# Ordering the additions of a mixture's output behind factors and scores on VectorE, at the start of an attention stage

## The chip, the cores and the metric

The kernel runs on one core of a Trainium2 chip. The metric is the device time of one execution in microseconds (us). The core has TensorE (PE in the profile, PEld for its weight loads), VectorE (DVE), ScalarE (ACT), GpSimd (POOL) and SyncE (SP); each works through its own queue of instructions in order.

## The reference, cut to what matters

The input `x` has 128 graphs of 64 nodes with 256 features, `adj` the edge weights. Two layers follow each other, each with a graph part and a feed-forward part that are added to `x`:

```python
x = x + _L0_gnn_ref(_layernorm(x, axis=-1), adj, ...)
x = x + _L0_ffn_ref(_layernorm(x, axis=-1), ...)      # 8 experts, the best one's output, times its probability
x = x + _L1_gnn_ref(_layernorm(x, axis=-1), adj, ...) # attention over a graph's 64 nodes
x = x + _L1_ffn_ref(_layernorm(x, axis=-1), ...)      # scores from 1,048,576 edges, then two of four experts
```

The change lies where the second line's sum meets the third line. Of the attention this is what counts here:

```python
Wh = jnp.matmul(h, W)
s1, s2 = Wh @ a1, Wh @ a2
e = s1[:, :, None] + s2[:, None, :]
e = jnp.where(e > 0, e, ALPHA * e)
e = jnp.where(adj > 0, e, NEG)
attention = jax.nn.softmax(e, axis=2)
h_prime = jnp.matmul(attention, Wh)
```

then a layer norm over the features and a gelu. `h` is the layer norm of `x`, so its mean and variance per node are needed before anything else of the attention can start.

## The kernel before, in words

The 8192 nodes are 64 tiles of 128 nodes by 256 features; `x` stays on chip as one array `[128, 64, 256]`. Four tiles make a group (`GR = 4`), so there are 16 groups (`NG`).

Layer 0's experts have written their rows to DRAM (`yrows`), in an order by expert. The function `back(g)` fetches the rows of a group's four tiles again with indirect DMAs issued by GpSimd (L1146, "gathers" here; one per tile, into tiles named `yin`, of which there are six, `by = GR + 2`), multiplies each with its node's probability and adds it to `x` (L1152, "additions" here), and takes the tile's statistics (L1138, `raw_stats`).

Layer 1's attention runs as a pipeline in steps `s`. In step `s` five functions work on five different groups, as generators that take turns: `back(s)`, `combine(s - 7)`, `tables(s - 10)`, `second(s - 5)` and `first(s - 4)`. With `PART = 2` the offsets are `FIRST = 4`, `SECOND = 5`, `COMBINE = 7`, `TABLES = 10`.

- `make_factors(i)` comes at the end of every second step. It turns the collected statistics of two steps into scales and shifts ("factors", tile `fac`): a chain of small VectorE instructions (L163 to L167, L1286, L154 to L159, L1290, L1291) of 128 x 24 elements. The first factors need the statistics of groups 0 and 1, the second those of groups 2 and 3.
- `first(g)` scales a group's tiles on ScalarE (L1037, tile `z`), transposes them on TensorE (L1168, `tz`), copies them (L1169, `zT`), multiplies by the weights (L1179, `pw`, copied to `wh` at L1182; L1186, `p2`), and makes the scores on VectorE (`ee`, five instructions, L1195 to L1208).
- `second(g)` does the softmax's exponential, a transpose and the product with `wh`, and takes statistics. `combine(g)` normalizes, applies gelu and adds to `x` (L1252). `tables(g)` prepares the second layer's feed-forward part, whose expert matrix products ("units", L1068 to L1082) are mixed in from step 12 on.

What is written above is the order in which the program is traced. The program's builder then makes each engine's queue from it: it plays the program through with durations of its own and puts, on each engine, an instruction that is ready before one that would have to wait, else the one traced earlier. So an addition of a later group can come to stand among the instructions of an earlier group's factors. `with tc.issue_after(ins):` tells the builder that the instructions traced inside, as far as they are on the engine of `ins`, have to come behind `ins` in that engine's queue. It adds no semaphore and no instruction. `made` is a dictionary in which the functions leave things for each other; `made["sent"]`, for instance, orders the loading of weights behind a step's store (L1316).

Of the kernel before, what the change touches and what calls it, by code (L numbers as in the profile page):

```python
# [15 lines left out]
ALU = mybir.AluOpType  # L16
# [4 lines left out]
P = 128  # L21
# [3 lines left out]
GR = 4  # L25
PART = 2


FIRST, SECOND, COMBINE, TABLES = 2 * PART, 2 * PART + 1, 3 * PART + 1, 4 * PART + 2
# [51 lines left out]
def kernel(  # L81
# [32 lines left out]
    V, S = nc.vector, nc.scalar  # L114
# [24 lines left out]
    x = const.tile([P, NT, D], F32, name="x")  # L139
# [12 lines left out]
    def root_of_bits(dst, v, guess, work):  # L152

        V.tensor_scalar(work.bitcast(I32), v.bitcast(I32), 1, None, ALU.logical_shift_right)  # L154
        V.tensor_scalar(guess.bitcast(I32), work.bitcast(I32), -1.0, float(0x5F3759DF), ALU.mult, ALU.add)
        for j in range(3):
            V.tensor_tensor(work, guess, v, ALU.mult)
            V.scalar_tensor_tensor(work, work, -0.5, guess, ALU.mult, ALU.mult)
            V.scalar_tensor_tensor(dst if j == 2 else guess, work, 1.5, guess, ALU.add, ALU.mult)  # L159

    def moments(raw, sm, df, var):

        V.tensor_tensor(sm, raw[:, :, :, 1], raw[:, :, :, 4], ALU.add)  # L163
        V.tensor_tensor(df, raw[:, :, :, 1], raw[:, :, :, 4], ALU.subtract)
        V.tensor_tensor(var, raw[:, :, :, 2], raw[:, :, :, 5], ALU.add)
        V.scalar_tensor_tensor(df, df, 0.25, df, ALU.mult, ALU.mult)
        V.scalar_tensor_tensor(var, var, 1.0 / D, df, ALU.mult, ALU.add)  # L167
# [21 lines left out]
    psel = const.tile([P, NT], F32, name="psel")  # L189
# [229 lines left out]
    with tc.tile_pool(name="w0", bufs=1, reuse_waits="tile") as w0, tc.tile_pool(name="kp", bufs=1, reuse_waits="tile") as kp:  # L419
# [29 lines left out]
        with tc.tile_pool(name="b2", bufs=2, reuse_waits="tile") as b2, tc.tile_pool(name="bh", bufs=NH + 2, reuse_waits="tile") as bh, tc.tile_pool(  # L449
# [4 lines left out]
            def transposed(zT, z, k):  # L454
                tz = psb.tile([P, GR * P], F32, name="tz")[:, 0:D].rearrange("p (c n) -> p c n", c=2)
                for c in range(2):
                    nc.tensor.transpose(tz[:, c, :], z[:, c * P : c * P + P], ident)
                S.copy(zT[:, :, k * P : k * P + P], tz)
# [16 lines left out]
            with tc.tile_pool(name="bg1", bufs=1, reuse_waits="tile") as bg1, tc.tile_pool(name="bg2", bufs=2, reuse_waits="tile") as bg2, tc.tile_pool(  # L475
# [58 lines left out]
                fac = bg1.tile([P, n_parts + 2, 4, M], F32, name="fac")  # L534
# [318 lines left out]
                V.tensor_tensor(past, past, tiles.unsqueeze(1).to_broadcast([P, NSLOT, E0]), ALU.mult)  # L853
                first = bg1.tile([P, NSLOT], F32, name="first")
                V.tensor_reduce(first, past, AX.X, ALU.add)
                V.tensor_tensor(iota_s, iota_s, first, ALU.subtract)
                V.scalar_tensor_tensor(es, es, float(NROW // P), iota_s, ALU.mult, ALU.add)
                V.tensor_scalar(es, es, 0.0, float(E0 * NROW // P - 1), ALU.max, ALU.min)
                last = V.tensor_copy(slot_t, es).ins

            with tc.tile_pool(name="bs", bufs=3, reuse_waits="tile") as bs, tc.tile_pool(
# [80 lines left out]
                for g in range(beside):  # L942
# [6 lines left out]
                    last = unit  # L949
# [166 lines left out]
    with ExitStack() as of_c:  # L1116
# [18 lines left out]
        made = {}  # L1135

        def raw_stats(norm, k, src):
            V.bn_stats(made["raw"][:, norm, s % PART * GR + k, :], src)  # L1138

        def back(g):  # L1140

            ys = []
            for k in range(GR):
                t = GR * g + k
                y = by.tile([P, D], F32, name="yin")
                nc.gpsimd.indirect_dma_start(  # L1146
                    y, None, yrows, bass.IndirectOffsetOnAxis(ap=row_y[:, t : t + 1], axis=0)
                )
                ys.append(y)
            for k in range(GR):  # L1150
                t = GR * g + k
                V.scalar_tensor_tensor(x[:, t, :], ys[k], psel[:, t : t + 1], x[:, t, :], ALU.mult, ALU.add)  # L1152
                raw_stats(0, k, x[:, t, :])
                yield

# [16 lines left out]
        def first(g):  # L1172
            zT = yield from transposed(g, 0)
            yield
            wh = whs[g % 2]
            for k in range(GR):
                pw = psc.tile([P, D + 1], F32, name="pw")
                for c in range(2):
                    nc.tensor.matmul(  # L1179
                        pw, zT[:, c, k * P : k * P + P], wx[:, c, :], start=(c == 0), stop=(c == 1)  # L1180
                    )
                S.copy(wh[:, k, 0 : D + 1], pw)  # L1182
            p2 = psc.tile([P, GR * P], F32, name="p2")
            for h in HALVES:
                for c in range(2):
                    nc.tensor.matmul(  # L1186
                        p2[h, 0 : GR * 64].rearrange("p (k j) -> p k j", j=64),
                        w2r[:, c, :],
                        zT[:, c, :].rearrange("p (k n) -> p k n", n=P)[:, :, h],
                        start=(c == 0),  # L1190
                        stop=(c == 1),
                    )
            yield
            ee = c2.tile([P, GR, 64], F32, name="ee")
            V.tensor_tensor(  # L1195
                ee,
                p2[:, 0 : GR * 64].rearrange("p (k j) -> p k j", j=64),
                wh[:, :, 0:1].to_broadcast([P, GR, 64]),
                ALU.add,
            )  # L1200
            V.scalar_tensor_tensor(ee, ee, 0.2, ee, ALU.mult, ALU.max)

            top = c1.tile([P, GR, 64], F32, name="top")
            V.tensor_scalar(top, on[:, GR * g : GR * g + GR, :], -2.0 * NEG, NEG, ALU.mult, ALU.add)
            V.tensor_tensor(ee, ee, top, ALU.min)
            m = c2.tile([P, GR], F32, name="m")
            V.tensor_reduce(m, ee, AX.X, ALU.max)
            V.tensor_tensor(ee, ee, m.unsqueeze(2).to_broadcast([P, GR, 64]), ALU.subtract)  # L1208
            made[g] = ee
            yield  # L1210

# [68 lines left out]
        def make_factors(i):  # L1280

            shape = [P, 3, PART * GR]
            raw = made["raw"]
            sm, df, ve, y, w = (c2.tile(shape, F32, name=f"mf{j}") for j in range(5))
            moments(raw, sm, df, ve)
            V.tensor_tensor(ve, ve, made["eps"], ALU.add)  # L1286
            fac = facs[i] = cf.tile([P, 3, 3, PART * GR], F32, name="fac")
            scale = fac[:, 0]
            root_of_bits(scale, ve, y, w)
            V.scalar_tensor_tensor(fac[:, 1], sm, -0.5, scale, ALU.mult, ALU.mult)  # L1290
            V.tensor_scalar(fac[:, 2], sm, 0.5, None, ALU.mult)  # L1291


        to.update(
# [9 lines left out]
        g, n = 0, -1  # L1304
        for s in range(n_steps):
            if s % PART == 0:
                made["raw"] = c2.tile([P, 3, PART * GR, 6], F32, name="raw")
                made["eps"] = c2.tile([P, 3, PART * GR], F32, name="eps")
                V.memset(made["raw"], 0.0)
                V.memset(made["eps"], EPS)  # L1310
            streams = []
            for of, by_steps in ((back, 0), (combine, COMBINE), (tables, TABLES), (second, SECOND), (first, FIRST)):
                if 0 <= s - by_steps < NG:
                    streams.append((of(s - by_steps), 2 if of == second and s % 2 else 0))
            if s == TABLES + 1:
                with tc.issue_after(made["sent"]):  # L1316
                    load_weights()

            r = 0
            while streams:  # L1320
                streams = [(st, at) for st, at in streams if at > r or next(st, s) is None]

                at = s - TABLES - 2
                if s >= NG + SECOND:
                    quota = int(r < 3)
                elif at >= 0:
                    quota = (2 * (at % 2), 2 * (at % 2), 4 - 4 * (at % 2), 0, 0, 0, 0, 0)[r]
                else:
                    quota = 0
                for _ in range(quota):  # L1330
                    g, n = next(units)
                r += 1
            if s % PART == PART - 1:
                make_factors(s // PART)
        while (n + 1) % (NH1 + GR):
            g, n = next(units)
# [255 lines left out]
    ahead = ctx.enter_context(tc.tile_pool(name="ahead", bufs=5, reuse_waits="tile"))  # L1592
# [354 lines left out]
    with tc.tile_pool(name="gd", bufs=1, reuse_waits="tile") as gd:  # L1947
        steps = gates(gd, 0, T0, {})
        for _ in sending:
            next(steps, None)  # L1950
            next(steps, None)
            g, n = next(units)
        for _ in steps:
            pass
        while (n + 1) % (NH1 + GR):
            g, n = next(units)
# [96 lines left out]
    with tc.tile_pool(name="fp", bufs=3, reuse_waits="tile") as fp:  # L2053


        moves = {0: send(1, sz), 1: back(0)}
        for n, h in enumerate(pairs()):
            if n % 3 == 2:
                next(moves[h], None)
            if n % 9 == 8:  # L2060
                next(stored, None)
    for _ in moves[1]:
        pass
    steps = back(PARTS - 1)
    for n, _ in enumerate(units):
        next(steps, None)
# [61 lines left out]
```

## Time and profile before

| | us |
|---|---|
| time before, median of 3 runs | 2247.34 (2247.14 to 2250.24) |
| the profiled execution: its own time | 2273.71 |
| its span, first to last instruction | 2272.0 |
| TensorE busy | 2081.2 (92%) |
| VectorE busy | 1522.8 (67%) |
| ScalarE busy | 921.7 (41%) |
| GpSimd busy | 448.6 (20%) |
| 64 gathers, L1146 | 64.3, from 1121.8 to 1305.6 |
| 64 additions, L1152 | 480 ns each (median), from 1125.5 to 1335.3 |

Times within the span count from its start. In the profile's lines, `x<-yin,psel,x` reads "writes x from yin, psel and x"; what stands in brackets after an instruction is how long its engine had been idle and what ended that. "remote" means that the profile has no sender for the semaphore that ended the wait; "issue" that it shows no wait at all. The attention stage starts at about 1118, and its last step's addition to `x` (L1252) is at 1479.7. The profiled execution is longer than the median of the runs by 26.4 us.

### The profile page before, as it was taken

The page shows a single profiled execution, that of the slowest core. Times are in us where ns is not written, and L with a number is a line of the kernel's source. Part 1 is how long each engine was busy: PE and PEld are TensorE (multiplying, and loading weights), DVE is VectorE, ACT ScalarE, POOL GpSimd, SP SyncE. Part 2 cuts the span into 40 slices and gives each one's busy share as a digit, 9 for nine tenths or more (in the row PEclk, how much of TensorE's full clock was granted, in tenths as well). Part 3 has the DMA queues.
Part 4 walks back from the last instruction along what each step waited for, and adds up shares of the span by engine and source line. Part 5 has one row for each costly group of instructions (what it writes and reads, how often), then busy time and mean ns, then how long its engine had stood idle before and what let it go on. Part 6 is the DMA issues. An engine that isn't in the chain of part 4 may idle for free. (4 is left out here: it accounts for less than half of the span.)

```text
span 2272.0 us, 31371 instructions
## 1 busy us (share of the span) xinstructions
PE 2081.2 (92%) x10046; PEld 1397.8 (62%) x10046; DVE 1522.8 (67%) x4539; ACT 921.7 (41%) x1662; POOL 448.6 (20%) x469
## 2 busy tenths in 40 slices
PE   7899999997999999999667889998999999999899
PEld 4444444443666666666445667665767767888776
DVE  6898988725899898893268665665788652323335
ACT  5767676663121121122046555531333342333322
POOL 2011101111000000000142200004556552213213
PEclk9999999998999999999878888998999999999999
DMA  8121112232111211112223311182222237878843
GB/s 223 31 68 59 49 55 68 83 98 77 55 35 53 61 32 54 54 32 72 59 67 103 95 33 43 66 245 62 60 57 50 58 117 219 281 239 263 251 144 105
DMA packets 206732, 219.84 MB, mean 97 GB/s; under 512 B 53200, under 2 KB 174416, under 8 KB 206560
## 3 DMA queue, kind: packets, MB, share of 16 engines
q1 hardware_dynamic: 181296, 182.37, 26.3%
q0 software_dynamic: 17056, 35.09, 5.6%
q8 instruction: 86, 1.41, 0.3%
q10 hardware_dynamic: 8208, 0.26, 0.2%
q14 instruction: 86, 0.70, 0.1%
HBM read 132.66 MB, written 84.91 MB: 96 GB/s over the span
## 5 line engine op out<-in xcount | busy, mean ns | idle before, releaser
L467 PE MATMUL ph<-zT,w 128*128 128x512 f32 x1056 | 507.2, 611 | 9.5 <-ACT zT L694 5.1
L470 ACT ACTIVATE hT<-ph,b 128x512 f32<-128x512 f32 x264 | 180.8, 687 | 501.0 <-PE ph L467 490.7
L467 PEld LDWEIGHTS ph<-zT,w 128*128 128x128 f32 x1056 | 190.1, 193 | 191.9 <-issue 168.8
L928 PE MATMUL py<-wd,hT 128*128 x1088 | 251.6, 383 | 0.0
L297 DVE TENSOR_TENSOR one<-iota_l,pb 128x1024 bf16<-128x1024 bf16 x192 | 234.3, 1220 | 1.2 <-PE cnt_ps L308 1.2
L928 PEld LDWEIGHTS py<-wd,hT 128*128 128x128 f32 x1088 | 200.8, 190 | 24.5 <-issue 0.5
L1540 POOL DMA_INDIRECT got<-tsrc,esrc x144 | 167.0, 1160 | 208.4 <-DVE esrc L1511 86.8
L1146 POOL DMA_INDIRECT yin<-yrows,row_y x64 | 64.3, 1005 | 693.7 <-SPq L991 573.3
L1078 PE MATMUL py<-w,hT 128*128 128x256 f32 x800 | 192.1, 391 | 9.1 <-DVE kt L1473 4.0
L1068 PE MATMUL ph<-zT,w 128*128 128x512 f32 x400 | 186.8, 609 | 0.0
L1078 PEld LDWEIGHTS py<-w,hT 128*128 128x128 f32 x800 | 150.9, 194 | 39.4 <-issue 13.9
L1072 ACT ACTIVATE hT<-ph,b 128x512 f32<-128x512 f32 x100 | 68.7, 688 | 212.5 <-PE ph L1068 193.6
L2004 PE MATMUL ph<-zTp,w1e 128*128 128x256 f32 x608 | 142.4, 389 | 12.2 <-DMA w1e<-in_L_ffn_W_dram 10.6
L2008 ACT ACTIVATE hT<-ph,b1e 128x256 f32<-128x256 f32 x152 | 71.7, 475 | 185.2 <-PE ph L2004 118.3
L2017 PE MATMUL py<-w,hT 128*128 x608 | 139.7, 383 | 2.8 <-DVE y L2025 2.5
L2004 PEld LDWEIGHTS ph<-zTp,w1e 128*128 128x128 f32 x608 | 118.4, 195 | 30.8 <-issue 11.9
L297 DVE TENSOR_TENSOR one<-iota_h,pb 128x512 bf16<-128x512 bf16 x192 | 131.7, 689 | 0.0
L620 PE MATMUL pre<-wd 128*128 128x512 f32 x256 | 126.9, 609 | 1.5 <-ACT wd L606 1.3
L1924 DVE SCALAR_TENSOR_TENSOR x<-yin,gate,x 128x256 f32<-128x256 f32 x108 | 52.1, 484 | 110.1 <-DMA yin<-ystore 105.4
L2017 PEld LDWEIGHTS py<-w,hT 128*128 128x128 f32 x608 | 113.8, 192 | 18.3 <-DVE y L2025 3.9
L308 PEld LDWEIGHTS <-one 128*128 128x128 bf16 x1536 | 69.4, 98 | 84.9 <-issue 59.7
L1068 PEld LDWEIGHTS ph<-zT,w 128*128 128x128 f32 x400 | 74.6, 194 | 73.2 <-issue 72.0
(414 smaller groups left out, 3468.6 us busy)
## 6 DMA issues: line engine op xcount, KB each, us to landing
w1e<-in_L_ffn_W_dram SPq DMA_DIRECT2D x38, 512.0 KB
yin<-ystore SPq DMA_DIRECT2D x24, 512.0 KB
ystore<-y SPq DMA_DIRECT2D x80, 128.0 KB
zslots<-none SPq DMA_DIRECT2D x38, 256.0 KB
zin<-zslots SPq DMA_DIRECT2D x38, 256.0 KB
yslots<-y SPq DMA_DIRECT2D x76, 128.0 KB
zin<-zrows SPq DMA_DIRECT2D x68, 128.0 KB
bd<-in_L_ffn_bd_dram SPq DMA_DIRECT2D x68, 128.0 KB
```

The costliest lines, as they stand in the source:

```text
L297: V.tensor_tensor(o, wi.unsqueeze(1).to_broadcast([P, HK, n]), pb[:, g : g + HK].unsqueeze(2).to_broadcast([P, HK, n]), ALU.is_equal,)
L308: nc.tensor.matmul(self.ps, one[0][:, k, :], one[1][:, k, :], start=(at + k == 0), stop=(at + k == n_chunks * KEPT - 1),)
L467: nc.tensor.matmul(ph, w1[:, c, q * P : q * P + P], zT[:, c, :], start=(c == 0), stop=(c == 1))
L470: gelus.append(S.activation(hT, ph, AF.Gelu, bias=b1[:, q : q + 1]).ins)
L620: nc.tensor.matmul(pre, xnT[:, c, n * P : n * P + P], wcat[:, c, :], start=(c == 0), stop=(c == 1),)
L928: nc.tensor.matmul(py, hTs[q][:, k * P : k * P + P], wd[:, bass.ds(ex[k], 1), q, :].rearrange("p e f -> p (e f)"), start=(q == 0), stop=(q ...
L1068: nc.tensor.matmul(ph, w1[:, e, c, q * P : q * P + P], zT[:, c, :], start=(c == 0), stop=(c == 1))
L1078: nc.tensor.matmul(py, hTs[q][:, k * P : k * P + P], w2[:, e, q, :], start=(q == 0), stop=(q == NH1 - 1))
L1540: nc.gpsimd.indirect_dma_start(got, None, tsrc, bass.IndirectOffsetOnAxis(ap=esrc[:, b, at : at + 1], axis=0))
L2004: nc.tensor.matmul(ph, w1e[:, c, q * P : q * P + P], zT[:, c, :], start=(c == 0), stop=(c == 1))
L2008: pace[:] = [S, S.activation(hT, ph, AF.Gelu, bias=b1e[:, q : q + 1]).ins]
L2017: nc.tensor.matmul(py, hTs[q][:, k * P : k * P + P], w2[:, e, q, :].rearrange("p e f -> p (e f)"), start=(q == 0), stop=(q == NH1 - 1),)
```

## The change

The additions of groups 2 to 8 are put under `issue_after`: those of groups 2, 3 and 4 behind the last factors traced so far, those of groups 5 to 8 behind the last scores traced so far. By the steps, that is the first factors for groups 2 and 3, the second for group 4, and the scores of group `g - 5` for group `g` from 5 to 8. Groups 0 and 1 and those from 9 on are left free. Two lines keep the instructions in `made`. The gathers are on GpSimd and get no order; but a gather needs one of six tiles, which an addition sets free.

```diff
@@ back(g), after its four gathers @@
+            if PART <= g <= FIRST:
+                ahead = made["factors"]
+            elif FIRST < g <= 2 * FIRST:
+                ahead = made["scores"]
+            else:
+                ahead = None
             for k in range(GR):
                 t = GR * g + k
-                V.scalar_tensor_tensor(x[:, t, :], ys[k], psel[:, t : t + 1], x[:, t, :], ALU.mult, ALU.add)
+                with tc.issue_after(ahead) if ahead is not None else ExitStack():
+                    V.scalar_tensor_tensor(x[:, t, :], ys[k], psel[:, t : t + 1], x[:, t, :], ALU.mult, ALU.add)
                 raw_stats(0, k, x[:, t, :])
                 yield
@@ first(g), the last of the score instructions @@
-            V.tensor_tensor(ee, ee, m.unsqueeze(2).to_broadcast([P, GR, 64]), ALU.subtract)
+            made["scores"] = V.tensor_tensor(ee, ee, m.unsqueeze(2).to_broadcast([P, GR, 64]), ALU.subtract).ins
@@ make_factors(i) @@
-            V.scalar_tensor_tensor(fac[:, 1], sm, -0.5, scale, ALU.mult, ALU.mult)
+            last = V.scalar_tensor_tensor(fac[:, 1], sm, -0.5, scale, ALU.mult, ALU.mult)
             V.tensor_scalar(fac[:, 2], sm, 0.5, None, ALU.mult)
+            made["factors"] = last.ins
```

## The prediction

> **What bounds the kernel now.** I read the engine windows first, then the waits, then the timeline of VectorE. Over the whole span TensorE is busy 92%, so only time in which it stands still can be won. The change touches one place, the start of layer 1's attention, and there TensorE does stand still. In the windows, the columns are PE, PEld, DVE, ACT and POOL busy (with counts), granted clock, DMA share, GB/s:
>
> ```profile
> core 0: us, PE busy (x) PEld busy (x) DVE busy (x) ACT busy (x) POOL busy (x), PEclk, DMA share, GB/s
> 1177.00:1220.00 43.00, 35.77 (x174) 25.21 (x172) 41.30 (x145) 33.88 (x71) 10.78 (x10) 0.92 0.11 32
> 1118.00:1177.00 59.00, 19.31 (x68) 11.74 (x69) 31.15 (x118) 13.18 (x27) 35.23 (x36) 0.62 0.30 87
> 1117.00:1149.20 32.20, 0.00 (x0) 0.00 (x0) 17.41 (x64) 0.63 (x2) 20.95 (x22) 0.58 0.33 96
> ```
>
> TensorE does nothing for 32.2 us (last row). POOL is then busy 20.95 us issuing 22 gathers. Further on, 1177 to 1220, VectorE is full: 41.30 of 43.00 us. The waits of 1118 to 1150 name who is waited for:
>
> ```profile
> ACT z L1037 <- DVE eps L1310: 44.7, 1, 44.7
> PE tz L1168 <- ACT z L1037: 32.3, 1, 32.3
> DVE x L1152 <- DMA yin<-yrows,row_y: 10.3, 9, 5.6
> ```
>
> TensorE's first transposes wait for ScalarE's scaling (L1037), and that for a memset (L1310) which stands just behind the last instruction of the first factors (L1290). So the factors are what is late. VectorE itself waited 10.3 us for gathers. Its timeline shows where:
>
> ```profile
> 1136.00 0.18 DVE L163 TENSOR_TENSOR mf<-raw 128x24 f32<-128x24 f32 x1
> ...
> 1137.46 0.48 DVE L1152 SCALAR_TENSOR_TENSOR x<-yin,psel,x 128x256 f32<-128x256 f32 x1 [0.40 <-DMA yin<-yrows,row_y]
> ...
> 1139.99 0.48 DVE L1152 SCALAR_TENSOR_TENSOR x<-yin,psel,x 128x256 f32<-128x256 f32 x1 [0.56 <-DMA yin<-yrows,row_y]
> ...
> 1142.57 0.48 DVE L1152 SCALAR_TENSOR_TENSOR x<-yin,psel,x 128x256 f32<-128x256 f32 x1 [0.62 <-DMA yin<-yrows,row_y]
> ...
> 1147.76 0.18 DVE L1290 SCALAR_TENSOR_TENSOR fac<-mf,fac 128x24 f32<-128x24 f32 x1 [1.75 <-remote]
> ```
>
> The factors of groups 0 and 1 start at 1136.00 and end at 1147.94. In between stand additions 9 to 15 (counted from 0), which belong to groups 2 and 3. Each is held until its gather lands, and gathers come one per 1.26 us (POOL starts at 1137.21, 1138.48, 1139.74).
>
> **What the Trainium skill says.** "DMA: Bandwidth & Descriptors", section "Anatomy of one DMA — SWDGE (gpsimd) path", gives a gather a fixed part of about 2.0 us plus its bytes; the trace agrees: the gather of 1125.69 is used by the addition at 1128.61, 2.9 us later, of which 1.1 us is POOL's own. "TensorE: Matmul & The Clock Gate", section "What's actually happening", says that TensorE runs at half clock after an idle window of about 3.4 us until it has been busy as long; the trace agrees (granted clock 0.58 in the idle row, 0.92 in the busy one). So an earlier start also ends the slow clock earlier; I count nothing extra for it.
>
> **The change, part by part.** No instruction is added or taken away. 28 of the 64 additions (groups 2 to 8) get an order on VectorE only. Groups 2 and 3 go behind the first factors, group 4 behind the second factors, groups 5 to 8 behind the scores of groups 0 to 3. All of these orders bind: by the windows of L1152, 9 additions ran before 1136, 7 more before 1147.9, 8 more before 1159.4 (end of the second factors), 2 before the first scores end (1164.4 begins the last of their instructions), 5 before the second's (1180.0), 2 and 4 before the third's and fourth's: 31 by 1180, 37 by 1200.2. Now at most 8 may run before the first factors end, 16 before the second, and 20, 24, 28 and 32 before the first, second, third and fourth scores.
>
> *First factors.* Addition 7 starts at 1133.72 and takes 0.48; its statistics (L1138, 0.42) end at about 1134.7. A chain of factors has 19 instructions. Undisturbed, its last ten run at 0.216 us each (a later chain in the timeline: 1492.76 to 1494.88). The first four depend on nothing in the chain and take 0.11 each, the other five I price like the last: 4 x 0.11 + 15 x 0.216 = 3.7. So they end at 1138.4 instead of 1147.94: **9.5 us earlier**, and TensorE's first transposes come at 1139.7 instead of 1149.2. If the 1.75 us stall before L1290 comes back, 7.8.
>
> *What waits behind.* Additions 8 to 13 run from 1138.4; their gathers have landed or are in flight. Gather 14 needs the buffer of addition 8 (six buffers), so 1139 at the earliest; it went at 1139.74 anyway. So POOL loses nothing here, and has no other work until 1441. SyncE gets no new wait. Addition 15 comes at about 1144, the second factors at 1144.5 + 3.7 = 1148.2 against 1159.4: 11.2 earlier. Additions of group 4 follow until 1151.3. The first scores need TensorE's chain, 1149.2 to 1164.8 before (15.6): now 1139.6 + 15.6 = 1155.2 at the latest, 9.6 earlier.
>
> *Additions behind scores.* These take work out of VectorE's idle stretch and put it into its full one. One addition with its statistics takes 0.40 + 0.37 = 0.77 at the pitch of 1191.6 to 1195.1. At the second scores 24 are done instead of 31 (7 late, 5.4 us); at the fourth 32 instead of 37 (5 late, 3.9 us). VectorE is 96% busy from 1177 to 1220, so the most that this can cost is 5.4. The least is nothing: from 1149.2 to 1177 VectorE idled 27.80 - 14.16 = 13.6 us, and if the scores follow each other quickly there is room for the moved work between them. Fillers also stretch the chain of five score instructions, from 2.1 us of work to 3.1 (1161.7 to 1164.8); without them each gets up to 1.0 back. I take 2 us of cost. The cover is idle VectorE time before step 7; without it the 5.4 applies.
>
> *Gathers.* They move with the buffers: group 5's third and fourth additions free buffers for group 6's last ones only after the first scores. A refill of two takes 2 x 1.26 + 2.9 = 5.4 us. The scores came 15.6, 10.7 and 9.5 us apart, so I cost this at nothing, 0 to 5 us.
>
> *Sum.* -9.5 + 2 = **-7.5 us**, between -11 (no cost, 11.2 at the second factors) and +1 (-7.8, +5.4, +3 for a late gather). The profiled execution took 2273.71 us (span 2272.0), 26.4 over the median of 2247.34; -7.5 makes it 2266. I put the same difference on the median, **2239.8**: the waits counted are mostly gathers' pitch, which is work of POOL. What the profile may add here are the stalls put down to "remote" (VectorE 5.4, ScalarE 7.2 us, all between 1146 and 1174), which I did not count as gained.
>
> **Does the head start last to the end?** The chain of waits reaches back only to 1548. After 1300 TensorE is busy 90.8 of 100 and then 95.4 of 100 us; nothing there has a date of its own, and the loading of weights (L1316) is itself ordered behind an attention step. So I let it shift whole.
>
> **The rivals.**
> *More than that.* The stalls of 1146 to 1174 lie in the thick of the gathers. If pacing gathers takes away some of them (ScalarE's 4.4 and 2.8), the gain is 9.5 + 7.2 less 0 to 2: 2231 to 2233. For it: they occur nowhere else. Against: VectorE's came while POOL idled, too. Chance 0.20.
> *About the same.* The program's builder orders all instructions by its own clock; a changed start reshuffles what follows, and a few us are given back between 1220 and 1300, where TensorE is busy 65.3 of 80: 2245. Chance 0.17.
> *Slower.* One mechanism: an addition behind scores stands in VectorE's order before its gather has landed, and the scores and statistics behind it wait. Its price is up to 5.4 us for each of groups 5 to 8; it decides once scores follow each other within 5.4 + 3.1 = 8.5 us. The gaps before were longer, but the first included stalls. Half of it in four groups is 11, with 5.4 for moved work, less 9.5: +7, 2254. Chance 0.17.
> *The order does not bind.* The counts above exclude it.
>
> **How the numbers follow.** My forecast, -7.5, has 0.46; with the larger gain, faster by over 0.2% (4.5 us, about what a measurement of this kernel can tell from no change) has 0.66. Same 0.17, slower 0.17. The range runs from the larger gain's 2231, a little below it, to the zero end of the sum and part of the slower case: 2230 to 2251. The likeliest case alone: 2236 to 2243.
>
> **What would show it.** Right: the first factors run without additions inside and end within 4 us of their start; the row L1152 <- DMA falls well below 10.3 us; TensorE's idle stretch is some 9 us shorter; 24 additions at the second scores. Wrong: additions of groups 5 to 8 waiting for DMA between 1155 and 1200 (the slower rival), or a later step such as L1252's last (1479.7) not moved by 5 us or more (head start lost).

## The result, and the profile after

| | before | after |
|---|---|---|
| median of 9 runs each, us | 2248.09 | 2240.14 |
| lowest to highest, us | 2244.28 to 2255.81 | 2233.34 to 2244.97 |
| ratio, 95% interval | | 0.9961 (0.9944 to 0.9978) |
| the profiled execution: time, span, us | 2273.71, 2272.0 | 2244.57, 2242.9 |

The kernel became 8.0 us faster in these runs. In two later sets of runs, on different chips, the full change came to 0.9974 as it is, and to 0.9966 with one transfer moved that turned out not to matter.

The page of the kernel after, its first lines:

```profile
span 2242.9 us, 31370 instructions
PE 2075.3 (93%) x10046; PEld 1394.6 (62%) x10046; DVE 1525.5 (68%) x4539; ACT 920.9 (41%) x1662; POOL 447.3 (20%) x469
```

The two spans differ by 29 us, but that is not the change: a second profile of the kernel before, shown below, has a span of 2243.5. The profile that the prediction rests on was a disturbed execution. So I read after against the second profile of before. The waits of before (second profile) from 1118 to 1146, columns engine, line and what is waited for, then us in total, times, longest:

```profile
ACT z L1037 <- DVE fac L1290: 40.9, 1, 40.9
PE tz L1168 <- ACT z L1037: 28.5, 1, 28.5
DVE x L1152 <- DMA yin<-yrows,row_y: 10.3, 11, 5.7
```

The waits of after from 1118 to 1140 (the added lines shift L1152 to L1161, L1168 to L1177, L1252 to L1261, L1290 to L1299):

```profile
ACT z L1037 <- DVE fac L1299: 34.6, 1, 34.6
PE tz L1177 <- ACT z L1037: 22.3, 1, 22.3
DVE x L1161 <- DMA yin<-yrows,row_y: 8.0, 5, 5.8
```

TensorE's wait fell from 28.5 to 22.3. VectorE still waits 8.0 us for gathers, but 5.8 of that is the first gather of all, which nothing could hide. Why TensorE waits less is in VectorE's timeline of after:

```profile
1134.84 0.20 DVE L163 TENSOR_TENSOR mf<-raw 128x24 f32<-128x24 f32 x1
...
1138.06 0.18 DVE L159 SCALAR_TENSOR_TENSOR fac<-mf,mf 128x24 f32<-128x24 f32 x1
1138.28 0.18 DVE L1299 SCALAR_TENSOR_TENSOR fac<-mf,fac 128x24 f32<-128x24 f32 x1
1138.38 0.87 DVE L1161 SCALAR_TENSOR_TENSOR x<-yin,psel,x 128x256 f32<-128x256 f32 x2
```

The first factors run from 1134.84 to 1138.46, 3.6 us, with no addition inside; the additions of group 2 follow at 1138.38. The windows of after, columns as in the prediction:

```profile
core 0: us, PE busy (x) PEld busy (x) DVE busy (x) ACT busy (x) POOL busy (x), PEclk, DMA share, GB/s
1117.00:1139.20 22.20, 0.00 (x0) 0.00 (x0) 12.55 (x50) 0.62 (x2) 13.24 (x14) 0.61 0.34 92
1177.00:1220.00 43.00, 29.25 (x116) 19.75 (x117) 41.94 (x142) 30.35 (x58) 14.98 (x15) 0.77 0.17 52
```

TensorE's idle stretch is 22.20 us long where it was 32.20 in the first profile of before and 28.5 in the second. VectorE is as full afterwards (41.94 of 43.00) as it was. The change reaches further than VectorE. With VectorE's queue the builder also changed those of ScalarE (another instruction in 94 positions) and TensorE (80 matmuls), all between 1148 and 1281 in this profile, as both profiles show when they are read instruction by instruction. GpSimd's and SyncE's queues are as before, and from 1281 on the queues of all engines are. No run changes VectorE's order alone.

What comes of the head start is seen stage by stage. The stages below run from the first transposes to the last score instruction of step 7 (the fourth scores), from there to step 11's (the eighth), to step 15's (the twelfth), and to the last addition of the attention. Windows of before, second profile:

```profile
1145.48:1186.13 40.65, 36.70 (x164) 24.05 (x164) 36.20 (x133) 28.85 (x63) 24.46 (x25) 0.91 0.29 83
1186.13:1249.74 63.61, 48.52 (x223) 36.99 (x224) 54.85 (x183) 43.23 (x81) 12.91 (x13) 0.80 0.41 128
1249.74:1340.81 91.07, 82.86 (x367) 61.62 (x365) 57.41 (x192) 52.72 (x95) 8.64 (x8) 0.84 0.15 49
1340.81:1466.02 125.21, 116.48 (x529) 83.29 (x528) 80.86 (x283) 70.03 (x125) 0.59 (x3) 0.92 0.16 53
```

The same stages in a second profile of after:

```profile
1138.82:1181.74 42.92, 36.89 (x164) 24.48 (x164) 39.05 (x138) 29.16 (x63) 24.75 (x25) 0.93 0.27 78
1181.74:1245.49 63.75, 50.77 (x224) 36.86 (x224) 55.11 (x183) 43.94 (x82) 17.79 (x17) 0.79 0.40 122
1245.49:1337.15 91.66, 81.63 (x365) 60.65 (x364) 60.80 (x201) 52.15 (x95) 8.76 (x9) 0.87 0.18 60
1337.15:1458.67 121.52, 112.81 (x529) 80.31 (x528) 80.59 (x282) 69.98 (x125) 0.59 (x3) 0.94 0.16 55
```

The first three stages are longer than before by 2.3, 0.1 and 0.6 us, so that 3.0 us of the head start are taken back. This fits the moved additions: VectorE has more work in the first stage (39.05 us, 36.20 before) and in the third (60.80, 57.41 before). The last stage is shorter by 3.7, with the same 529 matmuls in the same order, and TensorE is idle in it for 8.7 us as before. What differs is the granted clock, 0.94 where it was 0.92, and with it the matmuls' busy time, 112.81 where it was 116.48. So the gain at the attention's end is made of two parts of nearly equal size, and only one of them was foreseen.

### The profile page after: what moved, and what is told of

It is laid out like the page before. It is cut to its first block, busy times and chain, and to the rows that moved or that the text cites. A ratio compares the mean times of both kernels' runs of the same rounds, so it can differ in the third digit from the quotient of the medians.

```text
span 2242.9 us, 31370 instructions
## 1 busy us (share of the span) xinstructions
PE 2075.3 (93%) x10046; PEld 1394.6 (62%) x10046; DVE 1525.5 (68%) x4539; ACT 920.9 (41%) x1662; POOL 447.3 (20%) x469
## 5 line engine op out<-in xcount | busy, mean ns | idle before, releaser
L467 PEld LDWEIGHTS ph<-zT,w 128*128 128x128 f32 x1056 | 190.5, 193 | 192.8 <-issue 168.4
L750 POOL DMA_INDIRECT zrows<-z,pos x64 | 63.7, 995 | 281.6 <-issue 95.3
```

Source lines behind the costliest of these rows:

```text
L467: nc.tensor.matmul(ph, w1[:, c, q * P : q * P + P], zT[:, c, :], start=(c == 0), stop=(c == 1))
```

## The experiments

Two theories stood against each other at first. The first is the prediction's: the gain is the head start of the first factors, less a little for moved additions, so ordering groups 2 to 4 behind factors should bring most of it alone. The rival is that a changed order reshuffles what follows, and that the size of a gain comes from there; then parts don't add up.

Times are compared with the kernel before in the same set of runs. The attention stage does not start at the same time in all profiles (the last matmul of layer 0 ends between 1110.97 and 1118.22, though the instructions up to there are the same), so the table counts from that matmul's end in each profile and shows the difference to the second profile of before, in us; minus is earlier. So one unedited profile of before is the zero of every row. "T" is the start of the first transposes; S1, S4, S8 and S12 are the start of the last instruction of the first, fourth, eighth and twelfth scores; "end" is the attention's last addition to `x`.

| kernel | ratio, 95% interval | T | S1 | S4 | S8 | S12 | end |
|---|---|---|---|---|---|---|---|
| after, first profile | 0.9961 (0.9944 to 0.9978) | -6.3 | -4.5 | -3.9 | -3.6 | -2.9 | -6.6 |
| after_again | 0.9974 (0.9966 to 0.9983) | -5.9 | -4.3 | -3.7 | -3.5 | -2.9 | -6.6 |
| after_load_early | 0.9966 (0.9956 to 0.9977) | -6.4 | -4.5 | -3.9 | -3.6 | -2.9 | -6.6 |
| first_factors | 0.9987 (0.9977 to 0.9996) | -6.7 | -5.5 | -6.6 | -4.2 | -3.2 | -3.4 |
| free_four_load_late | 0.9981 (0.9971 to 0.9992) | -6.1 | -5.6 | -3.9 | +1.3 | +0.7 | +1.6 |
| factors_to_8 | 0.9999 (0.9989 to 1.0010) | -6.7 | -4.7 | -3.8 | -0.7 | -2.0 | -1.3 |
| all_groups | 1.0002 (0.9990 to 1.0013) | -6.2 | -4.5 | -3.8 | +0.5 | +1.3 | +2.0 |
| all_groups_load_late | 1.0004 (0.9991 to 1.0017) | -6.3 | -4.6 | -3.9 | +0.5 | +1.3 | +2.0 |
| scores_only | 1.0018 (1.0008 to 1.0027) | +0.1 | -0.6 | +1.7 | +0.6 | +0.7 | +0.3 |
| factors_only | 1.0025 (1.0014 to 1.0037) | -6.8 | -0.7 | -2.0 | +1.9 | +1.2 | -1.3 |
| factors_again | 1.0025 (1.0013 to 1.0037) | -6.5 | -0.5 | -1.4 | +7.2 | +2.9 | +2.8 |
| factors_load_late | 1.0029 (1.0016 to 1.0041) | -6.1 | -0.1 | -1.1 | +1.3 | +0.6 | -1.9 |

**before_again**: the kernel before, unedited, for a second profile.

> The kernel before, unchanged, against itself: ratio 1.000 within 0.002. It tells how far two profiles of one kernel differ. If the late semaphores between 1146 and 1174 us of the first profile (remote and issue waits, some 17 us over VectorE, ScalarE and TensorE) belong to the kernel, they come again, the last score of group 1 stands near 1180 us again and the attention's last addition (L1252) near 1479.7. If they were a disturbance of that one execution, they are gone, the group 1 score stands near 1168 and the last addition 8 to 14 us earlier than 1479.7, while the first factors still end near 1146 to 1148 with additions among them.

Ratio 0.9999 (0.9989 to 1.0008); profiled at 2245.24 us. The stalls that the first profile put down to "remote" (five waits, 12.6 us, between 1117 and 1180) are not in it, nor in either profile of after. They were that execution's own. The first factors end at 1144.71 instead of 1147.94.

**factors_only** and **factors_again**: groups 2 to 4 behind the factors, groups 5 to 8 free.

```diff
             if PART <= g <= FIRST:
                 ahead = made["factors"]
-            elif FIRST < g <= 2 * FIRST:
-                ahead = made["scores"]
             else:
                 ahead = None
```

> Only the additions of groups 2 to 4 are ordered (behind the first and second factors); those of groups 5 to 8 are free as before. On VectorE 8 additions stand before the first factors' end, 19 before the second's, 23, 26, 30 and 34 before the first to fourth scores. Theory (the first factors were held by gathers; the rest is small): 7 to 10 us faster than before, 2238 to 2241, first factors end near 1138.4, and within 2 us of the full change. Rival (pacing additions and gathers behind scores is what pays): at most 4 us faster than before.

> Groups 2 to 4 behind factors alone, once more, for a second profile: its first stood at 2239.9, while most runs stood at 2253 to 2257. Theory 1 (a side effect: in this kernel the builder puts SyncE's first load of zT ahead of the weights' loads, which the full change and the other two parts do not have): again 1.001 to 1.004 of before, and a profile of about 2254 in which the attention's last addition is within 3 us of the first profile's 1464 and the loss lies in one place behind it. Theory 2 (moved gathers and additions cost in the attention itself): the last addition comes 8 us or more later than 1464. Theory 3 (the first result was chance): 0.996 to 0.999.

Slower, twice: 1.0025, where the theory had 7 to 10 us faster. The head start came (T 6.5 to 6.8 us earlier), and was nearly gone at the first scores. VectorE's timeline of factors_load_late, a later run with the same VectorE order, shows why:

```profile
1146.27 0.18 DVE L157 TENSOR_TENSOR mf<-mf,mf 128x24 f32<-128x24 f32 x1
1149.82 0.48 DVE L1162 SCALAR_TENSOR_TENSOR x<-yin,psel,x 128x256 f32<-128x256 f32 x1 [3.36 <-DMA yin<-yrows,row_y]
1150.22 0.17 DVE L158 SCALAR_TENSOR_TENSOR mf<-mf,mf 128x24 f32<-128x24 f32 x1
...
1157.52 0.40 DVE L1218 TENSOR_TENSOR ee<-ee,m 128x256 f32<-128x256 f32 x1
```

In the middle of the second factors stands an addition of a free group (by its place it must be one of group 5 or later, since group 4's stand behind these factors). It holds VectorE for 3.36 us until its gather has landed, the next one for 0.70, and the first scores behind them come 4 us later than with the full change (1157.52; 1153.57 in after_again). This is the mechanism of the prediction's slower rival, in the place where groups 5 to 8 are free instead of behind scores. The order behind scores keeps these additions out of the second factors. It explains what is lost up to the first scores, but not the whole result: the attention ends at -1.3 and +2.8 us, while the kernel is some 6 us slower. For factors_again the ratio came as its first theory had it, but not the profile, which stood at 2245.07 in place of about 2254.

**scores_only**: groups 5 to 8 behind scores, groups 2 to 4 free.

```diff
-            if PART <= g <= FIRST:
-                ahead = made["factors"]
-            elif FIRST < g <= 2 * FIRST:
+            if FIRST < g <= 2 * FIRST:
                 ahead = made["scores"]
```

> Only the additions of groups 5 to 8 are ordered (behind the scores of groups 0 to 3); 16 additions stand before the first factors' end, as before, then 20, 20, 24, 28 and 32 before the second factors and the first to fourth scores. Theory (factors held by gathers): first factors end near 1147 as before, TensorE's first transposes near 1149; -2 to +3 us against before, where the plus would be the moved additions' cost of up to 5.4 us that the prediction took at 2. Rival (pacing pays): 4 to 9 us faster than before.

1.0018, about 4 us slower and a little outside the -2 to +3 that were expected. Without the factors' part there is no head start (T +0.1), and the scores of step 7 come 1.7 us later. VectorE's waits of scores_only from 1138 to 1160:

```profile
DVE ee L1202 <- PE p L1193: 4.4, 1, 4.4
DVE x L1159 <- DMA yin<-yrows,row_y: 2.2, 4, 0.7
```

VectorE now stands still for 4.4 us before the first scores, with additions kept back that it could have done there. Both parts alone make the kernel slower; together they make it faster. Here, too, the attention ends nearly level with before (+0.3), so that the 4 us are not explained by it.

**first_factors**: only groups 2 and 3, behind the first factors.

```diff
-            if PART <= g <= FIRST:
+            if PART <= g < 2 * PART:
                 ahead = made["factors"]
-            elif FIRST < g <= 2 * FIRST:
-                ahead = made["scores"]
```

> Only the additions of groups 2 and 3 are ordered, behind the first factors; 8 additions before the first factors' end, 22 before the second's, 22, 26, 30 and 33 before the first to fourth scores. Theory: nearly all of the gain stands in the first factors alone: 6 to 10 us faster than before; the second factors end some 2 to 4 us later than with the full change, which TensorE does not see while it works on groups 0 and 1. Rival (each factor chain that is freed pays for itself): half of the full change's gain, 3 to 5 us.

0.9987, about 3 us faster, where the theory had 6 to 10 and its rival 3 to 5. It leads the full change up to S12 (6.6 us against 3.8 at S4), and so shows that the order of groups 2 and 3 alone brings the whole head start. But its last stage is as slow as before's, and there the full change passes it: -3.4 against -6.6 at the end.

**after_again**: the full change, unedited, for a second profile on another chip.

> The changed kernel again, now on the chip and beside the runs of before that its parts are compared with. 5 to 10 us faster than before (0.9955 to 0.9980). Its profile against the second one of before: first factors 6 us earlier, the attention's last addition (L1261, L1252 before) 5 to 8 us earlier, and the end some 0 to 10 us earlier, where the part after 1850 moves both ways between executions.

0.9974, 5.3 us. Its marks agree with the first profile within 0.4 us everywhere, the 3.7 us of the last stage included.

**factors_to_8** (groups 2 to 8 all behind the latest factors) and **all_groups** (scores' order carried on to group 15):

```diff
-            if PART <= g <= FIRST:
+            if PART <= g <= 2 * FIRST:     # factors_to_8; its scores branch goes
-            elif FIRST < g <= 2 * FIRST:
+            elif FIRST < g:                # all_groups
```

> Groups 5 to 8 also ordered, but behind the latest factors in place of the latest scores: 8, 16, 20, 24, 28 and 32 additions before the first and second factors and the first to fourth scores, the same counts as the full change. SyncE's first load of zT stands ahead of the weights here too. If the counts (pacing) make the gain: like the full change, 5 to 9 us faster than before. If the place of that load on SyncE costs what it seems to cost with groups 2 to 4 alone: 0 to 8 us slower than before in spite of the same counts.

> The full change carried on: groups 9 to 15 behind the latest scores as well. Counts as the full change up to the fourth scores, then 36, 40, 44, 48, 52, 56, 60 before the fifth and following ones instead of 38, 44, 47, 49, 53, 61, 63. If additions that run ahead of their step disturb the steps in the middle too: 2 to 6 us faster than the full change. If only the start has idle engines to win: within 3 us of the full change, or slower by up to 6 where SyncE's load of zT stands ahead of the weights here as well.

Both are level with before, and all_groups is some 6 us behind the full change (2246.50 against 2240.18). factors_to_8 has as many additions ahead of each of the first four scores as the full change (20, 24, 28 and 32), so these counts alone do not make the gain. Both have the head start, keep it to S4 as the full change does, and lose it between S4 and S8. In the built queues these two and factors_only had one thing in common that the full change doesn't have: the builder had put the first load of `zT` (L1052) ahead of the loads of weights on SyncE. Was that the loss? The last runs were made to tell.

**factors_load_late** and **after_load_early**: the load's place alone is exchanged. In the first it goes behind the weights again, with every other engine's order that of factors_only; in the second it goes ahead of them, with every other order that of the full change.

```diff
@@ factors_load_late @@
-            nc.sync.dma_start(t, row(of).to_broadcast(t.shape))
+            loaded[:] = [nc.sync.dma_start(t, row(of).to_broadcast(t.shape)).ins]
...
-        nc.sync.dma_start(zTs[g].rearrange("p c n -> p (c n)"), zts[g])
+        with tc.issue_after(loaded[0]) if g == 0 else ExitStack():
+            nc.sync.dma_start(zTs[g].rearrange("p c n -> p (c n)"), zts[g])
@@ after_load_early: prepare(0, to) is traced ahead of load_weights() @@
-            if g == 0:
+            if g == 0 and 0 not in zTs:
...
+                prepare(0, to)
```

> The part that orders groups 2 to 4 behind the factors and leaves groups 5 to 8 free, with one thing put back: the first zT load of attention stands on SyncE behind the weights' last load again, as it does in the kernel before and in the full change. All other engines' orders are those of that part (measured twice at 1.0025 of before). Theory A, the early load is what takes back the head start between steps 7 and 11: 0.997 to 0.999 of before (2239 to 2243 us against 2246), and the scores of step 7 end at least 4 us sooner than they did with the early load, at 1244 to 1247 us. Theory B, the free additions of groups 5 to 8 between the factors' end and the scores take it back: 1.002 to 1.003, with step 7 at 1250 us or later. Theory C, clock alone decides and the order of loads is nothing: the time follows the granted clock, with no step between this and the part with the early load.

> The full change with one thing moved: the first zT load of attention is issued on SyncE ahead of the weights' loads and of the factors' store. All other engines' orders are those of the full change (0.9961 and 0.9974 of before). Theory A, the early load costs: 1.000 to 1.002 of before (2246 to 2250 us), the loss of 4 to 8 us lying between the scores of steps 3 and 7. Theory B or C, the load's place is nothing: 0.996 to 0.998, and step 7's scores 3 to 4.5 us ahead of the kernel before.

The load was not it. With the load late, the kernel of factors_only stays at 1.0029; with the load early the full change stays at 0.9966, and its windows are those of the full change to 0.3 us:

```profile
1182.03:1245.94 63.91, 50.92 (x224) 36.87 (x224) 55.28 (x184) 43.96 (x82) 17.94 (x17) 0.79 0.42 130
1337.66:1459.24 121.58, 112.85 (x529) 80.30 (x528) 80.64 (x283) 70.00 (x125) 0.59 (x3) 0.94 0.16 55
```

So the theory of the early load falls in both directions.

**all_groups_load_late** and **free_four_load_late** were tries for a better version, each with the load late; free_four has groups 2 and 3 behind the first factors, 5 to 8 behind scores, and 4 free:

```diff
-            if PART <= g <= FIRST:
+            if PART <= g < 2 * PART:
                 ahead = made["factors"]
             elif FIRST < g <= 2 * FIRST:
                 ahead = made["scores"]
```

> The ordering behind scores carried on to group 15 (1.0002 of before where the builder had put the first zT load early), with that load behind the weights again. Theory A: 0.995 to 0.998 of before, step 7's scores 4 us or more ahead of before, level with the full change or a little better. Theory B or C: 1.000 again, with the loss between steps 3 and 7 still there (step 7 no more than 1 us ahead of before).

> A candidate for the better version: groups 2 and 3 behind the first factors, group 4 free, groups 5 to 8 behind scores, the first zT load behind the weights. The part with groups 2 and 3 alone was 0.9987 of before and had the earliest scores of step 3 (8 us ahead of before); the order behind scores keeps the free groups from landing inside steps 4 to 8. If the head start of the first factors is the gain and the later order keeps it: 0.995 to 0.997. If moved additions only shift the work on VectorE: 0.998 to 1.000.

Neither beats the full change (1.0004 and 0.9981). For free_four, 0.995 to 0.997 was expected if the head start is kept, and 0.998 to 1.000 if not. Its window from S4 to S8:

```profile
1176.29:1245.04 68.75, 54.47 (x224) 39.22 (x224) 58.37 (x192) 45.35 (x84) 17.06 (x16) 0.78 0.42 126
```

and of all_groups_load_late:

```profile
1180.90:1248.95 68.05, 53.17 (x222) 39.00 (x222) 54.45 (x181) 42.37 (x80) 16.59 (x16) 0.75 0.42 126
```

From S4 to S8 the full change needs 63.8 us, with 55.1 us of VectorE work. free_four has 58.4 us of VectorE work there, because more additions fall into this stage, and needs 5.0 us more. But only 1.3 of the 5.0 is longer idle time of TensorE; the other 3.7 is longer busy time of its 224 matmuls (54.47 us, 50.77 in after_again). all_groups_load_late needs 4.3 more with no more VectorE work, at a clock of 0.75. And factors_only and factors_again, which are the same kernel with the same VectorE work there (58.6 and 58.9 us), need 67.5 and 72.2 us, at clocks of 0.80 and 0.72. So more work on VectorE goes with a lost head start in this stage, but the clock alone can cost as much, and the runs do not separate the two.

The last stage has the same 529 matmuls in all of them. Its length goes with the clock:

| granted clock, S12 to the end | length, us | kernels |
|---|---|---|
| 0.94 | 121.5, 121.6, 121.6 | the three profiles of the full change |
| 0.93 | 122.7, 122.7 | factors_only, factors_load_late |
| 0.92 | 124.8 to 125.2 | before (both profiles), first_factors, scores_only, factors_again |
| 0.91 | 125.9 to 126.1 | factors_to_8, all_groups (both), free_four |

factors_only and factors_again stand in different rows though they are the same kernel: the clock of this stage is not fixed by the kernel alone. The order of work does not explain it either: from about 1330 on TensorE and VectorE have the same order of instructions in all fourteen profiles, and TensorE is idle for 8.7 us of this stage in each.

The difference between before and after lies in one place of it. Windows of before_again there:

```profile
1391.00:1395.00 4.00, 3.28 (x15) 2.44 (x16) 4.00 (x19) 1.70 (x5) 0.00 (x0) 0.57 0.31 131
1395.00:1402.00 7.00, 7.00 (x28) 6.33 (x28) 2.76 (x10) 1.80 (x4) 0.00 (x0) 0.52 0.06 8
```

and of after_again:

```profile
1387.00:1391.00 4.00, 3.18 (x15) 2.40 (x16) 4.00 (x19) 1.71 (x5) 0.00 (x0) 0.57 0.32 131
1391.00:1398.00 7.00, 7.00 (x45) 6.03 (x45) 5.49 (x19) 5.00 (x9) 0.00 (x0) 1.00 0.06 9
```

In the first 4 us both do the same: 15 matmuls, 19 VectorE instructions, a clock of 0.57. Then TensorE is busy without a gap in both; after has the full clock at once and issues 45 matmuls in 7 us, before is at 0.52 and issues 28. In the clock records of all these profiles the granted clock is either 0.5 or 1 of full speed, and every stretch of 0.5 that ends within the profile lasts a whole multiple of 3.41 us. At this place it is three such steps in before_again and one in after_again:

```profile
1391.54:1401.78 10.24, 9.73 (x40) 8.37 (x39) 6.22 (x26) 2.85 (x6) 0.00 (x0) 0.50 0.16 57
1387.39:1390.80 3.41, 2.90 (x14) 2.12 (x15) 3.41 (x15) 1.29 (x3) 0.00 (x0) 0.50 0.37 154
```

Two steps, 6.83 us, of busy TensorE at half clock are 3.4 us of work lost, an estimate from these lines that comes to nearly the whole of the 3.7. In the four profiles at 0.91 the stretch has four steps.

## Why the prediction was right, and where only its sum was

The time forecast was 2239.8, and 2240.14 came; the gain forecast was 7.5 us, and 8.0, 5.3 and 6.8 came in the three comparisons. The mechanism of the first factors was right. That the total came so close is luck: errors in the head start and in the cost were made up for by a gain that the prediction did not count. By its steps:

- *First factors, 9.5 us earlier.* They end at 1138.46; the forecast said 1138.4. The chain was priced at 3.7 us and took 3.6. But the 9.5 was counted from an execution in which this chain ended 3.2 us later than in the second profile of before, 1.75 of it in the stall at L1290. Against the second profile it is 6.2, and TensorE starts 5.9 to 6.4 us earlier. The mis-sized term is the starting point, 1147.94; the prediction's own lower value, 7.8, takes the stall away and is still 1.6 too large. One line was also read too broadly: of the seven additions among the factors, three wait for their gather, by 0.40, 0.56 and 0.62 us, and not each.
- *Second factors, 11.2 us earlier, at 1148.2.* They end at 1150.75 in after_again, 3.9 earlier than in the second profile of before. The chain begins at 1145.14, and the first scores' instructions, which by then are ready, are mixed into it; the forecast had it alone.
- *First scores by 1155.2 at the latest.* Their last instruction starts at 1153.57. It could have come sooner: the fillers that the step said would be gone are still there. VectorE's timeline of after_again:

```profile
1150.24 0.42 DVE L1216 TENSOR_REDUCE m<-ee 128x4 f32<-128x256 f32 x1
1150.58 0.17 DVE L1299 SCALAR_TENSOR_TENSOR fac<-mf,fac 128x24 f32<-128x24 f32 x1
1150.67 0.88 DVE L1161 SCALAR_TENSOR_TENSOR x<-yin,psel,x 128x256 f32<-128x256 f32 x2
1151.46 0.74 DVE L1138 BATCH_NORM_STATS2 raw<-x 128x6 f32<-128x256 f32 x2
1152.13 0.86 DVE L1161 SCALAR_TENSOR_TENSOR x<-yin,psel,x 128x256 f32<-128x256 f32 x2
1152.91 0.74 DVE L1138 BATCH_NORM_STATS2 raw<-x 128x6 f32<-128x256 f32 x2
1153.57 0.41 DVE L1217 TENSOR_TENSOR ee<-ee,m 128x256 f32<-128x256 f32 x1
```

  Between the maximum (L1216) and the subtraction (L1217), the last step of the scores, stand the four additions of group 4 with their statistics, 2.9 us. They were just released by the second factors. first_factors, where group 4 is free, reaches S1 1.0 to 1.2 us sooner.
- *Additions behind scores, 2 us, 0 to 5.4.* Within its range: 3.0 us are lost between T and S12, with 24 additions ahead of the second scores and 32 ahead of the fourth, as counted. But about 1.6 of it is there at S1 already, where group 4's additions stand, which are ordered behind factors; about 1.4 comes after. (At the pitch of 1191.58 to 1193.04 an addition with its statistics takes 0.73 us and not 0.77, so that the upper end is 5.1.)
- *Gathers, nothing, 0 to 5 us.* Right: from 1155 to 1200 no addition of after waits for a DMA. (In the profile before, GpSimd's next own work is at 1447.48 and not at 1441; nothing rests on it.)
- *"I count nothing extra" for the clock.* This step failed, and with it the opening sentence that only time in which TensorE stands still can be won. The last stage is 3.7 us shorter at a higher clock, in all three profiles of the full change, with no less idle time of TensorE. This makes up for a head start that was counted 3 us too large and a cost counted 1 too small.
- *It shifts whole.* True in part. The attention's end came 6.6 us earlier, and so did the first gathers of the next part (6.5 to 6.6). Beyond that the profiles differ by several us either way. before_again and after_again, each within 0.3 us of its median, differ by 5.6 us in span: 0.7 less before the attention, 6.6 less in it, and 1.8 more behind it.

Of its signs of being right, three came as stated: no addition in the first factors, 3.6 us for them, 24 additions at the second scores. TensorE's idle stretch is 10.0 us shorter than in the profile that the prediction had, but 6.3 shorter than in the second one; and VectorE's wait for gathers fell to 8.0 and not well below 10.3. Neither sign of being wrong came.

Of the rivals, "more than that" had no ground, since the stalls are not part of the kernel. "The order does not bind" is excluded by the timeline of the first factors. "About the same" names something real: factors_to_8 and both forms of all_groups keep the head start to S4, lose it by S8 and are level with before. The "slower" mechanism occurs, but in the part where groups 5 to 8 are left free. Of the two theories that the experiments began with, the head start is borne out for the first factors; but the parts do not add up, as the theory of the reshuffled order had it.

Two things stay open. The first is why the clock comes back 7 us sooner at this place after the full change, and not after first_factors, which reaches S12 as early. No run changes that place alone, and the orders there are the same. The second is how far the attention's end decides the kernel's time. free_four ends its attention 1.6 us later than before and is about 4 us faster; scores_only ends it level and is 4 us slower. The median of factors_only is 7 to 8 us above before's, while its attention ends about level (-1.9 to +2.8); its three profiles fell on executions 3 to 14 us faster than its median, so that this loss wasn't located.

## What to carry to other kernels

Before a stall is counted as something to win, take a second profile: what is not in it is not the kernel's. When work is ordered away from a late chain, look at what the builder puts in its place. With groups 2 to 4 ordered and the later ones free it was an addition whose data had not landed, and the head start was nearly gone at the first scores; with groups 2 and 3 alone it was still there (-5.5). Compare stages from their own starts, and set busy time beside the granted clock, before a gain is given to the edit that was made.

## What the runs showed of the hardware

The clock's part was not expected in this size. The Trainium skill, "TensorE: Matmul & The Clock Gate", section "What's actually happening", says that the window by which the clock is set runs freely and that the number of slow matmuls varies from run to run. Here the later of the two slow stretches in the last stage was 10.2 us in both profiles of before, which reach it 13.7 us apart, and 3.4 us in all three of the full change; but factors_only and factors_again, the same kernel, had 13.7 and 10.2. So a few profiles that agree do not show that a stretch belongs to the kernel. The prediction took from that section that TensorE has its full clock again once it has been busy for about 3.4 us. In before_again it had been busy without a gap since 1393.67 and got the full clock at 1401.78, 8.1 us later. The page puts the cost of ramps under 1% of a typical span; in this kernel 3.7 us of such a ramp, 0.16%, is about half of what the change brought.

Over the runs of these kernels, mean granted clock and time go together: within a kernel, 0.001 of clock goes with 1.7 us (r = -0.77 over the 228 runs). The runs of before_again had a mean of 0.9632 and those of after_again 0.9667, which by that slope is 6.1 us, more than the whole difference of their medians, 5.0. This can't be read as the clock being the cause of all of it: an idle stretch is itself a time of low clock (0.59 in before_again), and 6 us less of it raises the mean as well.
